# A decoder layer with a written-out instruction order: other priorities, and the rank-16 weights loaded later

## The chip, the core and the metric

The kernel runs on one core of a Trainium2 chip. Its time is the device time of one execution in microseconds (us); the median of several runs is compared. The engines of the core that matter here are TensorE (PE; its weight loads are listed as PEld), VectorE (DVE), ScalarE (ACT), GpSimd (POOL) and SyncE (SP), which only issues DMAs here. Each engine works through its own instructions strictly in order and waits at an instruction until the semaphores that it needs are there. ScalarE issues a few DMAs too, in line with its arithmetic.

## The reference

One decoder layer on x of 8 x 512 x 256 with a context of the same shape, in float32. Three blocks follow each other, each with a residual and a layer norm:

```python
x = layernorm(x + attn(x))            # chunked linear attention: chunks of 32, decay mask, sigmoid gate, W_o
x = layernorm(x + xattn(x, ctx))      # 16 heads of 64: softmax(q k^T / 8) v, then Wo + bo
x = layernorm(x + ffn(x))             # h = ternary(x, w_fc) + gate * (x v^T fast_b^T u^T); ternary(relu(h)^2, w_proj)
```

In the ffn, `v` is 16 x 256, `fast_b` 16 x 16, `u` 1024 x 16 and `gate` a number: the rank-16 path. The two ternary weight matrices are rounded to -1, 0 or 1 with a scale per row.

## The kernel before

**Number format.** Almost every matmul runs on float16 pairs: a float32 value is split into a high part (a cast, mostly on ScalarE) and a low part (a subtraction on VectorE or GpSimd), and three products (high-high, high-low, low-high) are added in PSUM.

**Stages.** The loop over the eight batches is flattened into 256 units `(b, p, qt)`: batch, head pair and a quarter of the 512 queries. For each unit, `scores` computes two heads' scores (tile `s`, two groups of half-row matmuls that run side by side), VectorE adds the mask and takes the row extremum (`nm`), and ScalarE exponentiates into `e`. `split_p` splits `e` into the high and low halves of `ph` (high on ScalarE or GpSimd, low on VectorE), and a DMA transpose on SP's queue turns two units' `ph` into `pT`. `attend` multiplies `pT` by the values into `av`, some four units later; after the fourth quarter, `of`, `oh` and a DMA transpose give `oT`.

Around the units other work is filled in by four fillers: `gen_kv`, `gen_q` and `gen_v` (tiles `pk`, `pq`, `pvv`, into `W` and `v`) for later head pairs; `gen_l0` for the first block of the next batch (`xa`, `pss`, `pv`, `pg`, `po`, `pp`, then layer norm, `xsa` and a DMA transpose to `x1T`); `load_ctx` (`ctxs` into `ctxh`, on GpSimd after batch 0); `gen_wo` and `gen_ffn` for the batch before (`pwo`, then `x2T`; `pz`, `ph` with a batch number, `r`, `rh`, `py`). At the boundary between two batches the new batch's `pk` and `pq` need `ctxh` and `x1T`, which GpSimd makes in the stretch in which it also makes the low halves `rh` of the ffn. The last batch ends in `wo_tail` (`pwl`) and two `ffn_tail` generators of 256 rows each (`pyl`, `rhl`), whose steps are interleaved by hand.

**The order.** The program is recorded, not issued: every operation becomes an `Op` with a priority (`prio`), the number of the unit beside which it was recorded plus an offset. `Recorder.schedule` (line 300) then simulates the engines with the durations of `cost` (line 254). At each free moment of an engine it takes the operation with the least priority whose inputs and buffers are ready; `REACH` (line 30) limits how far past the first ready candidate it looks, `STICK` and `HOLD` favour staying in half-row or full-row matmuls. The result is a fixed order for each engine. The offsets come from several tables: `LATE` by kind of work, `PULL` (how many matmuls a filler may add for each unit), `TP` (dates in the tail), and `OFF` (line 39), which adds an offset for an engine and the name of the written tile:

```python
        if self.prio >= 0 and outs:
            o.prio += OFF.get(engine + " " + re.split(r"[0-9_]", outs[0].t.name or "")[0], 0.0)
```

**Start and rank-16 weights.** At the start SP's queue loads `wqk`, `xs`, `w0s`, `ctxs`, `wqs`, rows and so on, while ScalarE's queue loads `ld`, `ident`, `dif`, `bq`, `bk`. `load_rank` (line 662, called at line 1249) has ScalarE's queue load `sv`, `ur`, `fb` and `gt` there too; `setup_ffn` (line 668) uses them in batch 0 to make `vst`, `uh`, `fbs`, `uT` and `ust`. All DMAs of both queues take their semaphores from one set of eight in turn, so an issue can wait until an earlier DMA has landed.

**Buffers.** Buffers come from rings: `pT` and `ph` (3 each, 128 x 4096 float16), `t4` (5), `tmp2` (4), and eight PSUM banks. In `ffn_tail` (line 1036) `rhl` for all eight steps is one whole `pT` or `ph` buffer.

Of the kernel before, what the change touches and what calls it, by code (L numbers as in the profile page):

```python
# [11 lines left out]
F16 = mybir.dt.float16  # L12
F32 = mybir.dt.float32
# [8 lines left out]
HID, RANK = 1024, 16  # L22
# [4 lines left out]
LAG = 4  # L27
BURST = 2
MARGIN = 0.0
REACH = 11.86  # L30
SPARE = 1
DLATE = 1.6
PTS = 3
PHS = 3
NWP = 4
TP = (-1.12, 2.0, 1.04, 3.04, 0.1, 5.1, 2.67)
STICK = 2.09
HOLD = 0.18
OFF = {"ACT th": -0.28, "ACT zst": -1.63, "ACT r": 0.81, "PE pTp": 1.99, "SP pT": 1.41, "ACT sph": 0.41, "DVE zf": 0.49, "PE ph": 0.16, "POOL ph": -1.37, "PE pwp": -0.46, "PE pTb": 2.45, "PE pb": 3.1, "POOL xh": 2.55, "ACT rh": 1.56, "PE pu": 0.39, "ACT row": 1.53, "PE po": -0.14, "PE pwl": 1.81, "SP xs": 0.62, "PE pss": -0.66, "DVE wqkv": -0.5, "DVE fct": -3.44, "ACT oh": -1.55, "DVE sp": 1.14, "POOL rhl": 0.12, "POOL oh": -0.82, "PE pyl": -0.58, "PE pz": -2.5, "PE pp": 0.13, "DVE mvb": -0.45}
HIGH = ("apaa", "paaa", "papp")  # L40
LATE = {"k": 0.0, "q": 0.0, "v": 0.53, "w": -0.48, "l": -0.41, "o": -0.91, "f": 0.31, "s": 0.0, "a": 0.91, "t": -0.55, "x": 0.31, "e": 0.0, "c": -1.28, "d": -0.95}
PULL = {"k": 4.41, "l": 2.62, "w": 3.61, "f": 4.71, "g": 4.5}

PASSES = ((0, 0), (0, 1), (1, 0))

# [109 lines left out]
class Recorder:  # L155
# [34 lines left out]
    def add(self, engine, method, args, kw):  # L190
        ins, outs = [], []
        for n, x in enumerate(args):
            if isinstance(x, View):
                (outs if n == 0 or (method == "tensor_tensor_reduce" and n == 7) else ins).append(x)
        for k, x in kw.items():
            if isinstance(x, View):
                (outs if k == "accum_out" else ins).append(x)
        o = Op()
        o.engine, o.method, o.args, o.kw, o.prio = engine, method, args, kw, self.prio
        if engine in ("DVE", "ACT") and method[:3] != "dma" and self.prio >= 0:  # L200
            src = ins[0].t if ins else None
            if method == "tensor_tensor_reduce":
                o.prio += LATE["t"]
            elif method == "activation" and args[2] == AF.Exp:
                o.prio += LATE["x"]
            elif src is not None and src.pool[:2] == "ps":
                o.prio += LATE["e"]
        if self.prio >= 0 and outs:
            o.prio += OFF.get(engine + " " + re.split(r"[0-9_]", outs[0].t.name or "")[0], 0.0)
        o.preds, o.succs, o.bufs, o.parts = {}, [], [], None  # L210
        self.cost(o, ins, outs)
        if self.joint is not None and self.joint:
            j = self.joint[0]
            j.parts.append(o)
            self.access(j, ins, outs)
            return o
        o.seq = len(self.ops)
        self.ops.append(o)
        self.access(o, ins, outs)
        if self.joint is not None:  # L220
            o.parts = [o]
            self.joint.append(o)
        return o
# [30 lines left out]
    def cost(self, o, ins, outs):  # L254

        n = max([int(np.prod(x.shape[1:])) for x in outs + ins] or [0]) if o.engine != "PE" else outs[0].idx.size
        psum = any(x.t.pool[:2] == "ps" for x in ins + outs)
        ones = sum(x.idx.size == 1 and x.t.free > 0 for x in ins)
        o.half, o.port = None, o.engine == "POOL"
        o.dma = o.method[:3] == "dma"  # L260
        if o.dma:
            x = (outs or ins)[0]
            if o.method == "dma_start_transpose":
                blocks = n / 128
                o.occ, o.lat = 0.1 * blocks + 0.4, 0.115 * blocks + 0.55
            else:
                size = {F32: 4, F16: 2}.get(x.t.dt, 1)
                o.occ, o.lat = 0.45, n * size * x.shape[0] / (380e3 if self.prio < 0 else 210e3) + (1.2 if size == 1 else 0.1)
        elif o.engine == "PE":
            o.occ = n / 2400 + 0.0025 if ins[0].t.dt is F16 else n / 200  # L270
            o.lat = o.occ + 0.17
            if ins[0].p1 - ins[0].p0 == 64:
                o.half = ins[0].p0
        elif o.engine == "DVE":
            lat = 0.145 + n * 1.042e-3
            if o.method == "tensor_tensor_reduce":
                o.occ, o.lat = 0.615, 0.8
                return
            if not psum and o.method in ("tensor_copy", "tensor_scalar") and n >= 512:
                lat = 0.12 + n * 0.62e-3  # L280
            if psum and ones and o.method == "scalar_tensor_tensor":
                lat += 0.065
            if n <= 8:
                lat = 0.19 if o.method == "reciprocal" else 0.175 if o.method == "bn_aggr" else 0.145
            o.occ, o.lat = lat - 0.085, lat
            o.port = not psum and o.method in ("tensor_tensor", "scalar_tensor_tensor", "tensor_scalar", "tensor_copy")
        elif o.engine == "ACT":
            lat = 0.165 + n * 0.83e-3 + (0.0 if psum else 0.04) + 0.07 * ones
            o.occ, o.lat = (lat + 0.01, lat + 0.12) if "accum_out" in o.kw else (lat - 0.11, lat)
        elif o.engine == "POOL":  # L290
            if o.method == "tensor_tensor":
                lat = 0.3 + n * 1.67e-3 if n <= 512 else 0.2 + n * 1.9e-3
                if o.args[3] == ALU.pow:
                    lat = 0.42 + 0.16 * n
            else:
                lat = 0.13 + n * 0.9e-3 if n > 512 else 0.92 if n == 256 and o.kw == {} and o.method == "tensor_scalar" and o.args[-1] == ALU.is_lt else 0.62 if n > 256 else 0.56 if n > 8 else 0.22 + n * 5e-3
            o.occ, o.lat = lat - 0.03, lat
# [178 lines left out]
def decoder_kernel(ctx: ExitStack, tc: tile.TileContext, ins: dict, out: bass.AP):  # L476
# [13 lines left out]
    def tmp2(name, shape, dt=F32):  # L490
        return wk.tile(shape, dt, tag="tmp2", name=name, bufs=4)
# [162 lines left out]
        nc.vector.tensor_scalar(th[:, 0:n], sc, 0.5, None, ALU.mult)  # L654
        nc.vector.tensor_scalar(th[:, n:2 * n], sc, -0.5, None, ALU.mult)

    sv = cst.tile([128, 2, RANK], F32, name="sv")
    ur = cst.tile([128, 8, RANK], F32, name="ur")
    fb = cst.tile([RANK, RANK], F32, name="fb")
    gt = cst.tile([128, 1], F32, name="gt")  # L660

    def load_rank():
        nc.scalar.dma_start(sv, ins["vT"].rearrange("(c p) r -> p c r", p=128))
        nc.scalar.dma_start(ur, ins["u"].rearrange("(c p) r -> p c r", p=128))
        nc.scalar.dma_start(fb, ins["fast_b"])
        nc.scalar.dma_start(gt, ins["gate"].broadcast_to([128, 1]))

    def setup_ffn():
        sfc = cst.tile([128, 8], F32, name="sfc")
        for i in range(2):  # L670
# [38 lines left out]
        yield 6  # L709

        nc.gpsimd.memset(vst, 0.0)
        split(vst[:, :, 0:RANK], vst[:, :, 96:96 + RANK], sv, WS)
        for g in (32, 64):
            nc.scalar.copy(vst[:, :, g:g + RANK], vst[:, :, 0:RANK])

        rs = cst.tile([128, 8], F32, name="rs")
        nc.vector.reciprocal(rs, sfc)
        nc.vector.tensor_scalar(rs, rs, gt, None, ALU.mult)
        nc.vector.tensor_tensor(ur, ur, rs.unsqueeze(2).broadcast_to([128, 8, RANK]), ALU.mult)
        uh = tmp2("uh", [128, 2, 8, RANK], F16)  # L720
        split(uh[:, 0], uh[:, 1], ur, 1.0)
        fbs = cst.tile([RANK, 2, 128], F16, name="fbs")
        nc.gpsimd.memset(fbs, 0.0)
        split(fbs[:, 0, 0:RANK], fbs[:, 1, 0:RANK], fb, 1.0)
# [311 lines left out]
    def ffn_tail(b, i, base, step_):  # L1036
        row = rows[b]
        rh, py = {}, {}
        ts = slice(256 * i, 256 * i + 256)

        rhl = wk.tile([128, 8, 2, 256], F16, tag=("pT", "ph")[i], name=f"rhl{i}", bufs=(PTS, PHS)[i])
        PL = 3
        for s_ in range(8 + PL):
            nc.prio = base + step_ * s_
# [2 lines left out]
            if s_ < 8:  # L1047
                j = s_
                r4 = ffn_h(b, j, ts, zst, f"{b}_{i}", True)
                hl = rhl[:, j]  # L1050
                if i == 0 or j % 2:
                    nc.scalar.activation(r4, r4, AF.Square)
                else:
                    nc.vector.tensor_tensor(r4, r4, r4, ALU.mult)
                if j % 2:
                    nc.scalar.copy(hl[:, 0], r4)
                else:
                    nc.vector.tensor_copy(hl[:, 0], r4)
                (nc.vector if j % 3 == 2 or (i == 1 and j == 7) else nc.gpsimd).tensor_tensor(hl[:, 1], r4, hl[:, 0], ALU.subtract)
                rh[j] = hl  # L1060
# [185 lines left out]
            setup_qkv(2, 0, N1, 0)  # L1246
            run_all(gen_v(0, 0))
    nc.prio = -1.0
    load_rank()
    for i in (1, 2, 0):  # L1250
        setup_qkv(i, N1, HID, 0)
    nc.prio = 0.0
# [3 lines left out]
    def at(i, off):  # L1256
        now[0], nc.prio = i, i + off
# [84 lines left out]
            if pend:  # L1342
                attend(pend.pop(0))

    at(U, TP[6])
    bf.drain()
    at(U, TP[0])
    rest(len(pend) - 4)
# [63 lines left out]
```

## Time and profile before

| | us |
|---|---|
| median of 3 runs (lowest, highest) | 1062.17 (1061.53, 1063.61) |
| profiled execution | 1060.95 |
| its span, first to last instruction | 1058.8 |
| PE, DVE, ACT, POOL busy | 994.6, 985.8, 884.5, 568.7 |
| idle of TensorE and VectorE, 548.2 to 671.9 (one batch) | 2.7, 6.6 |

The page gives busy time, share of the span and number of instructions of each engine, and slices of a fortieth of the span (26.5 us) whose digits are the busy share in tenths. A line of the timeline has start, duration, engine, source line, operation, output<-input and shapes, and in brackets the idle time before it with what ended that. Line 454 stands for every recorded operation, since all are issued there; tiles tell them apart. A busy TensorE is not one at its peak, because ends of pipelined matmuls are modelled.

### The profile page before, as it was taken

What the parts mean: (1) busy time and instruction counts of PE and PEld (TensorE: products, weight loads), DVE (VectorE), ACT (ScalarE), POOL (GpSimd) and SP (SyncE); (2) the same over time, 40 slices, a digit from 0 to 9 for tenths busy, and PEclk for the clock granted to TensorE, in tenths of its full rate; (3) what the DMA queues carried; (4) which work ended last, traced back from release to release, by engine and by line L of the source; (5) the groups of instructions that cost most, each with busy time, mean ns of one, the idle gap of its engine ahead of it and who ended that gap; (6) DMA issues with size and microseconds to landing.
All of it is one profiled execution on the core that took longest, in us unless ns stands there. A gap on an engine that the chain in (4) does not pass through costs nothing.

```text
span 1058.8 us, 29904 instructions
## 1 busy us (share of the span) xinstructions
PE 994.6 (94%) x11976; PEld 636.0 (60%) x11976; DVE 985.8 (93%) x2087; ACT 884.5 (84%) x1885; POOL 568.7 (54%) x518
## 2 busy tenths in 40 slices
PE   6987879999999999999999999999999999999996
PEld 4544545665666566765567656665567655565574
DVE  6998999999899989999899999999899998999886
ACT  6797978899986998789987899869987899878846
POOL 0255284256842587344952579425873449424646
PEclk9999999999999999999999999999999999999999
DMA  8359999999999999989999899999999899999971
GB/s 289 119 107 195 186 191 197 178 155 185 194 172 201 164 177 180 203 155 187 173 193 201 158 167 196 187 196 153 180 182 209 147 187 160 187 203 164 174 124 41
DMA packets 646635, 185.64 MB, mean 175 GB/s; under 512 B 628448, under 2 KB 641376, under 8 KB 646496
## 3 DMA queue, kind: packets, MB, share of 16 engines
q1 hardware_dynamic: 644144, 183.34, 94.5%
q8 instruction: 93, 1.52, 0.6%
q10 hardware_dynamic: 2352, 0.40, 0.2%
q14 instruction: 46, 0.38, 0.1%
HBM read 21.18 MB, written 4.19 MB: 24 GB/s over the span
## 4 chain that ended last, share of the span: by engine, by line
PE 48%; DVE 24%; POOL 8%; DMA 8%; ACT 5%; issue 5%; SPq 1%; ACTq 0%; POOLq 0%; DVEq 0%
PE s L454 9%; PE av L454 9%; DVE s L454 8%; DVE ph L454 6%; PE pwo L454 6%; PE pvv L454 5%; PE pk L454 4%; PE pq L454 4%; DMA pT<-ph 4%; PE py L454 3%; DVE W L454 2%; POOL xsa L454 2%; ACT e L454 2%; POOL row L454 2%; PE pxa L454 2%
## 5 line engine op out<-in xcount | busy, mean ns | idle before, releaser
L454 ACT ACTIVATE e<-s,nm 128x512 f32<-128x512 f32 x512 | 350.5, 696 | 79.8 <-DVE nm L454 72.2
L454 DVE SCALAR_TENSOR_TENSOR ph<-e,ph 128x1024 f16<-128x1024 f32 x256 | 334.6, 1310 | 22.7 <-ACT ph L454 20.5
L454 DVE CUSTOM_DVE_ANT_0 s<-s,mb 128x512 f32<-128x512 f32 x512 | 342.1, 706 | 11.0 <-PE s L454 10.0
L454 PEld LDWEIGHTS <-pT 128*128 128x128 f16 x6144 | 197.5, 98 | 60.6 <-issue 37.6
L454 PE MATMUL av<-v,pT 128*128 128x64 f16 x6144 | 212.3, 194 | 12.0 <-DMA pT<-ph 9.7
L454 PE MATMUL s<-W 64*128 64x512 f16 x1536 | 207.4, 379 | 10.7 <-ACT e L454 8.8
L454 ACT ACTIVATE ph<-e 128x1024 f16<-128x1024 f32 x186 | 198.2, 1071 | 2.0
L454 POOL TENSOR_SCALAR ph<-e 128x1024 f16<-128x1024 f32 x70 | 87.5, 1250 | 203.9 <-ACT e L454 187.7
L454 POOL TENSOR_TENSOR oh<-of,oh 128x512 f16<-128x512 f32 x62 | 99.3, 1602 | 92.3 <-ACT oh L454 86.6
L454 PEld LDWEIGHTS <-W 64*128 64x128 f16 x1536 | 64.6, 94 | 108.6 <-issue 53.9
L454 PEld LDWEIGHTS <-wqkv 128*128 128x128 f16 x768 | 68.6, 98 | 88.3 <-issue 27.2
L454 PE MATMUL pk<-ctxh,wqkv 128*128 128x512 f16 x384 | 97.9, 383 | 11.9 <-POOL ctxh L454 8.8
L454 ACT ACTIVATION_READ_ACCUMULATOR e<-s,nm 128x1 f32 x512 | 108.3, 211 | 0.0
L454 PE MATMUL pvv<-wqkv,ctxh 128*128 128x256 f16 x768 | 97.9, 274 | 0.2 <-ACT e L454 0.2
L454 PE MATMUL pq<-x1T,wqkv 128*128 128x512 f16 x384 | 96.1, 380 | 1.3 <-DVE x1T L454 0.7
L454 POOL TENSOR_TENSOR rh<-r,rh 128x512 f16<-128x512 f32 x56 | 76.1, 1367 | 21.2 <-ACT rh L454 20.7
L454 PEld LDWEIGHTS <-oT 128*128 128x128 f16 x768 | 73.4, 98 | 20.9 <-issue 4.8
L454 PEld LDWEIGHTS <-ctxh 128*128 128x128 f16 x768 | 72.8, 98 | 17.4 <-issue 5.9
L454 PE MATMUL pwo<-wo,oT 128*128 128x256 f16 x672 | 82.0, 273 | 0.8 <-ACT e L454 0.5
L454 DVE DVE_READ_ACCUMULATOR2_ANT nm<- 128x1 f32 x512 | 70.0, 137 | 0.0
L454 PE MATMUL ph<-x2T,tfc 128*128 128x512 f16 (+1 forms) x288 | 67.3, 355 | 0.3 <-DVE of L454 0.2
L454 PE MATMUL py<-tpj,rh 128*128 128x256 f16 x448 | 60.3, 273 | 1.3 <-ACT rh L454 1.2
(190 smaller groups left out, 1485.6 us busy)
## 6 DMA issues: line engine op xcount, KB each, us to landing
row<-in_x SPq DMA_DIRECT2D x8, 512.0 KB, 5.8
xs<-in_xT SPq DMA_DIRECT2D x7, 512.0 KB, 4.5
ctxs<-in_ctxT SPq DMA_DIRECT2D x7, 512.0 KB, 4.1
out_dram<-row SPq DMA_DIRECT2D x7, 512.0 KB, 3.5
wqs<-in_wqkv SPq DMA_DIRECT2D x6, 512.0 KB, 8.1
pT<-ph SPq DMA_TRANSPOSE x131, 7.6
wos<-in_wo SPq DMA_DIRECT2D x4, 256.0 KB, 3.2
fcs<-in_w_fc SPq DMA_DIRECT2D x2, 512.0 KB, 4.5
```

What stands on the lines that cost most here:

```text
L454: getattr(real[x.engine], x.method)(*[r(a) for a in x.args], **{k: r(a) for k, a in x.kw.items()})
```

## The change

The table `OFF` and its use go, so every operation's priority is that of its kind of work alone. `REACH`, `TP` (one date less; the drain of the fillers at the tail's start now is at unit number + 1 and not + 2.67), two entries of `LATE` and two of `PULL` get other values. `cost` no longer prices a float32 matmul apart. `load_rank` goes: `setup_ffn` loads `sv`, `gt`, `ur` and `fb` itself, on SP's queue, just ahead of their use in the program (where they land in the queue is up to the planner), `sv` and `ur` into `tmp2` buffers. The host lays `u` and `v` out per partition, so that each partition's values are one piece (512 and 128 bytes, before in pieces of 64 bytes). In `ffn_tail`, each step's `rhl` is a `t4` buffer of its own.

```diff
@@ -27,19 +27,18 @@
 LAG = 4
 BURST = 2
 MARGIN = 0.0
-REACH = 11.86
+REACH = 9.52
 SPARE = 1
 DLATE = 1.6
 PTS = 3
 PHS = 3
 NWP = 4
-TP = (-1.12, 2.0, 1.04, 3.04, 0.1, 5.1, 2.67)
+TP = (0.35, 0.96, 1.15, 3.0, 0.5, 5.1)
 STICK = 2.09
 HOLD = 0.18
-OFF = {"ACT th": -0.28, "ACT zst": -1.63, "ACT r": 0.81, "PE pTp": 1.99, "SP pT": 1.41, "ACT sph": 0.41, "DVE zf": 0.49, "PE ph": 0.16, "POOL ph": -1.37, "PE pwp": -0.46, "PE pTb": 2.45, "PE pb": 3.1, "POOL xh": 2.55, "ACT rh": 1.56, "PE pu": 0.39, "ACT row": 1.53, "PE po": -0.14, "PE pwl": 1.81, "SP xs": 0.62, "PE pss": -0.66, "DVE wqkv": -0.5, "DVE fct": -3.44, "ACT oh": -1.55, "DVE sp": 1.14, "POOL rhl": 0.12, "POOL oh": -0.82, "PE pyl": -0.58, "PE pz": -2.5, "PE pp": 0.13, "DVE mvb": -0.45}
 HIGH = ("apaa", "paaa", "papp")
-LATE = {"k": 0.0, "q": 0.0, "v": 0.53, "w": -0.48, "l": -0.41, "o": -0.91, "f": 0.31, "s": 0.0, "a": 0.91, "t": -0.55, "x": 0.31, "e": 0.0, "c": -1.28, "d": -0.95}
-PULL = {"k": 4.41, "l": 2.62, "w": 3.61, "f": 4.71, "g": 4.5}
+LATE = {"k": 0.0, "q": 0.0, "v": 0.53, "w": -0.33, "l": -0.41, "o": -0.91, "f": 0.31, "s": 0.0, "a": 0.91, "t": 0.0, "x": 0.31, "e": 0.0, "c": -1.28, "d": -0.95}
+PULL = {"k": 5.13, "l": 2.62, "w": 3.61, "f": 4.71, "g": 5.48}
 
 PASSES = ((0, 0), (0, 1), (1, 0))
 
@@ -205,8 +204,6 @@
                 o.prio += LATE["x"]
             elif src is not None and src.pool[:2] == "ps":
                 o.prio += LATE["e"]
-        if self.prio >= 0 and outs:
-            o.prio += OFF.get(engine + " " + re.split(r"[0-9_]", outs[0].t.name or "")[0], 0.0)
         o.preds, o.succs, o.bufs, o.parts = {}, [], [], None
         self.cost(o, ins, outs)
         if self.joint is not None and self.joint:
@@ -267,7 +264,7 @@
                 size = {F32: 4, F16: 2}.get(x.t.dt, 1)
                 o.occ, o.lat = 0.45, n * size * x.shape[0] / (380e3 if self.prio < 0 else 210e3) + (1.2 if size == 1 else 0.1)
         elif o.engine == "PE":
-            o.occ = n / 2400 + 0.0025 if ins[0].t.dt is F16 else n / 200
+            o.occ = n / 2400 + 0.0025
             o.lat = o.occ + 0.17
             if ins[0].p1 - ins[0].p0 == 64:
                 o.half = ins[0].p0
@@ -654,17 +651,6 @@
         nc.vector.tensor_scalar(th[:, 0:n], sc, 0.5, None, ALU.mult)
         nc.vector.tensor_scalar(th[:, n:2 * n], sc, -0.5, None, ALU.mult)
 
-    sv = cst.tile([128, 2, RANK], F32, name="sv")
-    ur = cst.tile([128, 8, RANK], F32, name="ur")
-    fb = cst.tile([RANK, RANK], F32, name="fb")
-    gt = cst.tile([128, 1], F32, name="gt")
-
-    def load_rank():
-        nc.scalar.dma_start(sv, ins["vT"].rearrange("(c p) r -> p c r", p=128))
-        nc.scalar.dma_start(ur, ins["u"].rearrange("(c p) r -> p c r", p=128))
-        nc.scalar.dma_start(fb, ins["fast_b"])
-        nc.scalar.dma_start(gt, ins["gate"].broadcast_to([128, 1]))
-
     def setup_ffn():
         sfc = cst.tile([128, 8], F32, name="sfc")
         for i in range(2):
@@ -709,16 +695,24 @@
         yield 6
 
         nc.gpsimd.memset(vst, 0.0)
+        sv = tmp2("sv", [128, 2, RANK])
+        nc.sync.dma_start(sv, ins["vT"].rearrange("p (c r) -> p c r", c=2))
         split(vst[:, :, 0:RANK], vst[:, :, 96:96 + RANK], sv, WS)
         for g in (32, 64):
             nc.scalar.copy(vst[:, :, g:g + RANK], vst[:, :, 0:RANK])
 
+        gt = cst.tile([128, 1], F32, name="gt")
+        nc.sync.dma_start(gt, ins["gate"].broadcast_to([128, 1]))
         rs = cst.tile([128, 8], F32, name="rs")
         nc.vector.reciprocal(rs, sfc)
         nc.vector.tensor_scalar(rs, rs, gt, None, ALU.mult)
+        ur = tmp2("ur", [128, 8, RANK])
+        nc.sync.dma_start(ur, ins["u"].rearrange("p (c r) -> p c r", c=8))
         nc.vector.tensor_tensor(ur, ur, rs.unsqueeze(2).broadcast_to([128, 8, RANK]), ALU.mult)
         uh = tmp2("uh", [128, 2, 8, RANK], F16)
         split(uh[:, 0], uh[:, 1], ur, 1.0)
+        fb = cst.tile([RANK, RANK], F32, name="fb")
+        nc.sync.dma_start(fb, ins["fast_b"])
         fbs = cst.tile([RANK, 2, 128], F16, name="fbs")
         nc.gpsimd.memset(fbs, 0.0)
         split(fbs[:, 0, 0:RANK], fbs[:, 1, 0:RANK], fb, 1.0)
@@ -1037,8 +1031,6 @@
         row = rows[b]
         rh, py = {}, {}
         ts = slice(256 * i, 256 * i + 256)
-
-        rhl = wk.tile([128, 8, 2, 256], F16, tag=("pT", "ph")[i], name=f"rhl{i}", bufs=(PTS, PHS)[i])
         PL = 3
         for s_ in range(8 + PL):
             nc.prio = base + step_ * s_
@@ -1047,7 +1039,7 @@
             if s_ < 8:
                 j = s_
                 r4 = ffn_h(b, j, ts, zst, f"{b}_{i}", True)
-                hl = rhl[:, j]
+                hl = t4(f"rhl{i}{j}", [128, 2, 256])
                 if i == 0 or j % 2:
                     nc.scalar.activation(r4, r4, AF.Square)
                 else:
@@ -1246,7 +1238,6 @@
             setup_qkv(2, 0, N1, 0)
             run_all(gen_v(0, 0))
     nc.prio = -1.0
-    load_rank()
     for i in (1, 2, 0):
         setup_qkv(i, N1, HID, 0)
     nc.prio = 0.0
@@ -1342,7 +1333,7 @@
             if pend:
                 attend(pend.pop(0))
 
-    at(U, TP[6])
+    at(U, 1)
     bf.drain()
     at(U, TP[0])
     rest(len(pend) - 4)
@@ -1391,8 +1382,8 @@
     a["bo"] = f("L0_xattn_bo").reshape(1, D)
     a["w_fc"] = f("L0_ffn_w_fc")
     a["w_proj"] = f("L0_ffn_w_proj")
-    a["u"] = f("L0_ffn_u")
-    a["vT"] = np.ascontiguousarray(f("L0_ffn_v").T)
+    a["u"] = np.ascontiguousarray(f("L0_ffn_u").reshape(8, 128, RANK).transpose(1, 0, 2).reshape(128, -1))
+    a["vT"] = np.ascontiguousarray(f("L0_ffn_v").T.reshape(2, 128, RANK).transpose(1, 0, 2).reshape(128, -1))
     a["fast_b"] = f("L0_ffn_fast_b")
     a["gate"] = f("L0_ffn_gate").reshape(1, 1)
     i = np.arange(128)
```

## The prediction

> **What bounds the kernel now.** I read the page's busy shares and slices first, then windows by stage, then the start and one batch boundary in the timeline.
>
> ```profile
> PE 994.6 (94%) x11976; PEld 636.0 (60%) x11976; DVE 985.8 (93%) x2087; ACT 884.5 (84%) x1885; POOL 568.7 (54%) x518
> PE   6987879999999999999999999999999999999996
> DVE  6998999999899989999899999999899998999886
> ```
>
> The slices have TensorE full from the seventh on; up to there VectorE is. The windows (us, then busy us of PE, PEld, DVE, ACT, POOL, clock, DMA share, GB/s) say how full:
>
> ```profile
> 48.00:92.00 44.00, 36.90 (x391) 20.79 (x389) 43.97 (x101) 38.14 (x92) 22.09 (x18) 0.97 0.66 120
> 92.00:164.00 72.00, 59.81 (x699) 35.19 (x696) 67.68 (x144) 56.69 (x123) 40.33 (x33) 0.97 1.03 192
> 1008.00:1027.00 19.00, 18.28 (x316) 15.92 (x314) 16.89 (x37) 8.93 (x22) 10.53 (x11) 1.00 0.92 149
> 1027.00:1058.80 31.80, 21.97 (x195) 16.23 (x191) 20.10 (x64) 20.23 (x51) 17.39 (x29) 0.95 0.10 34
> ```
> ```profile
> 548.20:671.90 123.70, 121.03 (x1481) 77.53 (x1479) 117.10 (x246) 106.34 (x223) 72.19 (x64) 1.00 1.03 181
> ```
>
> Batch 0 (to 164 us) is set by VectorE, the batches after it by TensorE. One such batch takes 123.7 us and TensorE stands still for 123.70 - 121.03 = 2.7 us of it; VectorE for 6.6. The tail is a chain with gaps on every engine. So a new order can win 2.7 us a batch at most, and lose more.
>
> **Part 1, the four rank-16 loads leave the start.** They are the last DMAs on ScalarE's queue, ahead of its table load:
>
> ```profile
> 5.05 0.39 ACTq L454 DMA_DIRECT2D sv<-in_vT  x1
> 6.91 1.28 ACT L454 ACT_TABLE_LOAD   x1 [6.91 <-DMA sv<-in_vT]
> 8.32 0.61 ACT L454 ACTIVATE wqkh<-wqk 128x512 f16<-128x512 f32 x1
> ```
>
> bk is issued at 2.62 and takes 0.45, so without sv, ur and fb the table load stands first at 3.07 and ends at 4.4; wqk lands 4.3 to 4.8 after its issue at 0.72, and wqkh can start at 5.1 to 5.5 instead of 8.32. The first matmul (9.88) follows 3 us sooner. The chain of waits has loads on the path next:
>
> ```profile
> 7.34 0.38 SPq L454
> ...
> 9.74 0.43 SPq L454
> ...
> 10.21 7.77 DMA wqs<-in_wqkv
> ```
>
> By the semaphores in the two instruction orders, each of these loads waits for the landing of the eighth DMA before it, counted over both queues. With four fewer in the count w0s waits for wqk and ident (5.1, 5.4) and no longer for wqk's second half and bq (6.0, 7.3), and the wqs that went out at 10.21 goes out near 8.7: 1.5 us sooner. VectorE is 27.72 of 28 us busy from 20 to 48 and 43.97 of 44 to 92, so what it gets sooner it keeps. Bounds -3.1 (ScalarE's step) and 0; I take -1.5, the load's step, because the chain runs through the load.
>
> **Part 2, the same loads later, on SP.** gt and fb go between two loads of rows that nobody awaits: 0. sv and ur are issued after the second tpj transpose, ahead of pT of head pair 3: two issues of 0.39 and 0.48 make +0.9. Behind sv on ScalarE stands the high half of ph (pair 4), behind ur on VectorE its low half; if landing (3.0 and 3.7 us at the start) isn't covered, both stand. Bounds 0 and +3.7; I take +0.8, as one score unit, a v and pwo work lie between. The layout in itself: ur's 64 KB landed in 3.7 us in pieces of 64 bytes; nobody waits for the bytes, 0. [...]
>
> **Part 3, batch 0 in another order.** The instructions are the same, and VectorE's work is. Its idle 4.3 us (92 to 164) is the most that can be won; as much again can be lost, since the largest TensorE stalls there are followed by a slow clock (below). No row tells which: 0, bounds -4 and +4. The planner's price for the one f32 matmul drops back; the trace has it as two of 0.39 us, once: 0.
>
> **Part 4, the batches in another order.** Without OFF, with REACH 9.52 and other PULLs, the two instruction orders differ in every batch alike. The work on TensorE is the same and so are the changes between half-row score groups and full-row groups (183 runs of scores before, 185 after). What differs is what lies between a result and its reader. At the boundary:
>
> ```profile
> 634.20 0.38 PE L454 MATMUL pk<-ctxh,wqkv 128*128 128x512 f16 x1 [0.50 <-POOL ctxh L454]
> 635.90 1.45 PE L454 MATMUL pk<-ctxh,wqkv 128*128 128x512 f16 x6 [1.22 <-POOL ctxh L454]
> ```
> ```profile
> PE pk L454 <- POOL ctxh L454: 1.7, 2, 1.2
> PEld L454 <- POOL rh L454: 1.0, 4, 0.4
> ```
>
> Before, one py matmul stands between pk's first matmul and the second; after, four ph, nine py, one pk and one pq do: 4 x 0.215 + 9 x 0.109 + 2 x 0.215 = 2.3 us, so the 1.2 and most of the 1.7 can go. Against that, py now follows its ph closer: from ph 4 to 7 to the py that reads them lie 9.2 to 10.1 us of matmuls, before 12.8 to 13.7 (by the same per-matmul times, 0.117 for a score matmul, 0.029 for av). Between them go relu, square and cast on ScalarE and a GpSimd subtraction of 1.2, and GpSimd is full there, with row (3.3), xsa (4.2), ctxh (3.5). At 13 us of cover the weight loads of py already waited 1.0 for rh. So a batch may win 1.7, or lose up to 3.6 of cover less the 1.2 = 2.4. I take +0.6, past the middle (+0.35), because x1T is also put ahead of a pT on SP's queue, and behind it stands the av that had 0.6 us to spare (pT issued at 630.54, landing 7.6 later, used at 638.7). Six boundaries with an ffn beside them: 6 x 0.6 = +3.6, bounds -10.2 and +14.4.
>
> **Part 5, the tail.** After the last score the old order still has 43 py matmuls of the batch before, the new one none: 4.1 us of matmuls less behind the last score and as much more ahead of it. Ahead, TensorE had 32 - 29.2 = 2.8 us idle (976 to 1008) to take it in. Behind, 18.28 of 19 us were busy, so most of it is won there. Net bounds -2.8 and +4.1; I take +0.5, near nothing. rhl moves from whole pT and ph buffers to five t4 buffers: rhl 15 on ScalarE now waits until pyl has read rhl 10, which is 11 pyl matmuls of 0.109 after ph 16, 1.2 us, of which one relu (0.42) covers a part: +0.7, bounds 0 and +1.2.
>
> **Sum.** -1.5 + 0.8 + 0 + 3.6 + 0.5 + 0.7 = +4.1 on the profiled execution's 1060.95 (span 1058.8 and 2.15 around it) gives 1065.1; the median of the runs is 1.2 above that execution, so 1066.3.
>
> **Rival 1, faster.** The wait for ctxh goes and the shorter cover for rh suffices: -0.7 a boundary, -4.2, with the start at -2 and the rest at 0: 1062.2 - 6.2 = 1056. For it: the boundary's wait is the largest that TensorE has in a batch, and the start's gain is plain in the trace. Against it: GpSimd is full exactly where the cover shrinks. It decides the other way once py waits more than 1.7 us a batch.
>
> **Rival 2, much slower.** The wait for rh or pT passes 2 us in each batch, and then the clock falls:
>
> ```profile
> 985.00:986.00 1.00, 0.43 (x4) 0.13 (x2) 1.00 (x1) 1.00 (x4) 1.00 (x2) 1.00 2.31 163
> 986.00:987.00 1.00, 0.00 (x0) 0.00 (x0) 1.00 (x2) 1.00 (x3) 1.00 (x1) 1.00 0.05 6
> 987.00:988.00 1.00, 0.53 (x11) 0.54 (x12) 1.00 (x4) 1.00 (x3) 0.66 (x1) 0.69 0.98 215
> 988.00:989.00 1.00, 1.00 (x10) 0.41 (x9) 0.07 (x2) 1.00 (x3) 0.93 (x1) 0.50 1.18 227
> ```
>
> About 2 us without a matmul, then 0.50 of the clock for some 3 us, that is 1.5 us lost. Six times 2.4 + 1.5 is 23 instead of 3.6: 1086; at three boundaries of six, 1076. [...] The row shows the drop after 2 us, so I keep the 1.5. Against it: the orders give every reader at least 9 us.
>
> **Rival 3, nothing to see.** The reordering is neutral and start and tail cancel: 1062.2, within the 0.2% (2.1 us) that a measurement of this kernel can tell from no change.
>
> **How the numbers follow.** Forecast (slower, 1064.3 to 1073) 0.56, rival 2 0.09, rival 1 0.27, rival 3 0.08. Hence slower 0.65, same 0.08, faster 0.27. The range for 8 in 10 reaches from rival 1's middle, 1056, to three boundaries of rival 2, 1076; the forecast's own range is 1063 to 1073.
>
> **What would show it.** Right or wrong, step by step: the table load near 3 us and the first pA matmul near 6.7; the chain's wqs issue near 8.7; no wait of pk for ctxh but longer ones of py, or PEld, for rh; a batch of 124.3 us where it was 123.7; no py after the last score, and ScalarE's rhl waiting for pyl. The prediction is wrong if a batch takes 123 us or less, or if idle time on TensorE in batch 0 moves by over 4 us.

## The result and the profile after

The changed kernel takes 1064.01 us (median of 22 runs), the one before 1062.13 on the same chip: ratio 1.0024, interval 1.0014 to 1.0033, that is 2.5 us slower (1.5 to 3.5). The ratio goes by all runs and is not the quotient of the two medians, which are 1.9 us apart. The forecast was 1066.3, slower. The profiled execution of the changed kernel took 1066.91 (span 1064.8), 2.9 above its median. Executions of one kernel lie up to some 5 us from its median, so below sizes come from these ratios with their intervals, each against the kernel before on the same chip, and profiles tell only where the time goes.

The page and the windows of the changed kernel, as they were shown of the kernel before:

```profile
PE 1003.9 (94%) x11976; PEld 641.8 (60%) x11976; DVE 985.0 (93%) x2087; ACT 882.3 (83%) x1885; POOL 555.8 (52%) x518
PE   7987878999999999999999999999999999998986
DVE  7999699999899989999899989999899998998976
```
```profile
92.00:164.00 72.00, 57.83 (x637) 32.65 (x637) 61.22 (x131) 51.47 (x115) 35.12 (x30) 0.88 0.95 177
548.40:672.10 123.70, 121.34 (x1487) 78.05 (x1484) 116.96 (x246) 106.08 (x223) 70.85 (x64) 1.00 1.04 182
1008.00:1027.00 19.00, 16.13 (x256) 13.02 (x253) 15.97 (x31) 7.98 (x22) 9.57 (x7) 0.91 1.13 188
```

Two places changed. In the fifth slice (106 to 133 us) VectorE falls from 9 to 6 tenths; from 92 to 164 us it now idles 72 - 61.22 = 10.8 us where it idled 4.3, and the clock is 0.88, not 0.97. And near the end TensorE has two slices at 8 (958 to 985 and 1011 to 1038 us) where all but the last were full. The stretch of 123.7 us in the steady batches looks as before; it has the length that one batch had before, and by the units below a batch of the changed kernel is shorter, 122.7 us on average for 123.4.

Where the time is gained and lost is read best from the order of the units. The table gives the start (us) of VectorE's first masking step `s<-s,mb` of some units, counted in the trace of each profiled execution; the kernels are those of the experiments below.

| first step of unit | 0 | 16 | 24 | 32 | 64 | 224 | 255 | end of span |
|---|---|---|---|---|---|---|---|---|
| before | 49.5 | 110.6 | 136.9 | 167.4 | 285.1 | 902.0 | 1010.4 | 1058.8 |
| after | 46.0 | 108.4 | 143.1 | 171.7 | 290.2 | 903.5 | 1013.5 | 1064.8 |
| e5 | 50.4 | 114.7 | 144.7 | 176.7 | 298.8 | 915.0 | 1023.5 | 1072.1 |
| e6 | 46.0 | 108.2 | 141.1 | 169.8 | 288.2 | 903.2 | 1011.5 | 1062.8 |
| e7 | 44.4 | 112.8 | 141.9 | 174.4 | 297.7 | 909.1 | 1017.8 | 1068.9 |
| e8 | 47.5 | 108.4 | 134.7 | 165.4 | 282.2 | 897.4 | 1006.0 | 1057.4 |
| f | 48.0 | 109.3 | 135.7 | 166.0 | 285.6 | 903.3 | 1011.5 | 1060.1 |

After against before: 3.5 us ahead at unit 0, 4.3 behind at unit 32, with 8.4 lost between units 16 and 24 alone (34.7 us for 26.3); from unit 64 to 224, five batches, 613.3 for 616.9; from unit 255 to the end 51.3 for 48.4. So the change seems to gain at the start and in the steady batches and to lose in batch 0 and in the tail; these are single executions, and the experiments say how much of it holds.

**The start** went as the prediction's Part 1 had it (timeline of the changed kernel, ScalarE and TensorE):

```profile
3.11 1.28 ACT L451 ACT_TABLE_LOAD   x1 [3.11 <-issue]
...
4.99 0.63 ACT L451 ACTIVATE wqkh<-wqk 128x512 f16<-128x512 f32 x1
...
6.63 0.59 PE L451 MATMUL pA<-wqkh,wqkh 128*128 128x256 f16 x2 [6.63 <-ACT wqkh L451]
```

The table load is at 3.11 instead of 6.91, the first matmul at 6.63 instead of 9.88, and the first decay step on VectorE (`sp`) 2.4 us sooner.

**Batch 0** has a hole. The chain of waits of the changed kernel runs through SP's queue there, and VectorE's timeline shows who stands:

```profile
107.82 1.28 SPq L451
...
109.20 3.29 DMA sv<-in_vT
```
```profile
109.05 0.73 DVE L451 CUSTOM_DVE_ANT_0 s<-s,mb 128x512 f32<-128x512 f32 x1
109.70 0.14 DVE L451 DVE_READ_ACCUMULATOR2_ANT nm<- 128x1 f32 x1
112.77 0.19 DVE L451 SCALAR_TENSOR_TENSOR vst<-sv,vst 128x32 f16<-128x32 f32 x1 [2.93 <-ACT vst L451]
```

The late `sv` is issued at 109.20, behind a transpose, and lands 3.29 us later; ScalarE and VectorE stand at `vst` until then, with `ph` of a unit queued behind it. VectorE stands for 2.93 us, and a slow clock follows (0.57, then 0.50); the load is not the whole of it, since in e6 below, where `sv` is early, VectorE still stands 1.04 us at this step, for ScalarE. Windows of 1 us, changed kernel (columns as in the prediction; the clock is the third number from the end):

```profile
109.00:110.00 1.00, 0.38 (x4) 0.10 (x1) 0.84 (x4) 0.71 (x3) 0.00 (x0) 1.00 2.54 149
110.00:111.00 1.00, 0.00 (x0) 0.00 (x0) 0.00 (x0) 0.73 (x3) 0.00 (x0) 1.00 0.06 7
111.00:112.00 1.00, 0.70 (x24) 0.71 (x25) 0.00 (x0) 0.00 (x0) 0.00 (x0) 1.00 0.81 167
112.00:113.00 1.00, 1.00 (x27) 1.00 (x24) 0.19 (x1) 0.49 (x2) 0.00 (x0) 0.57 0.74 160
...
121.00:122.00 1.00, 1.00 (x7) 0.47 (x6) 0.78 (x4) 0.84 (x3) 0.72 (x1) 0.50 0.00 0
122.00:123.00 1.00, 1.00 (x21) 0.78 (x20) 0.00 (x0) 1.00 (x4) 0.00 (x0) 0.80 0.00 0
```

TensorE stood for 1.92 us (to 111.30, for a `pT` transpose) and the clock was 0.57 and then 0.50 until 122.

**The steady batches.** The waits from 290 to 905 us, before and after:

```profile
PE pk L454 <- POOL ctxh L454: 8.1, 9, 1.2
...
PEld L454 <- POOL rh L454: 4.4, 18, 0.4
...
PE py L454 <- ACT rh L454: 1.0, 4, 0.3
```
```profile
PE pk L451 <- POOL ctxh L451: 3.1, 5, 0.7
```

The wait of `pk` for `ctxh` fell from 8.1 to 3.1 us, and the shorter way from `ph` to `py`, which the prediction feared, costs nothing: no wait of `py` for `rh` is left, nor of the weight loads for GpSimd's `rh` (for ScalarE's half they still wait 1.0 us in all, 2.4 before).

### The profile page after: what moved, and what is told of

Its sections match the earlier page's. It is cut to its first block, busy times and chain, and to the rows that moved or that the text cites. A ratio compares the mean times of both kernels' runs of the same rounds, so it can differ in the third digit from the quotient of the medians.

```text
span 1064.8 us, 29936 instructions
## 1 busy us (share of the span) xinstructions
PE 1003.9 (94%) x11976; PEld 641.8 (60%) x11976; DVE 985.0 (93%) x2087; ACT 882.3 (83%) x1885; POOL 555.8 (52%) x518
## 4 chain that ended last, share of the span: by engine, by line
PE 38%; DVE 22%; ACT 16%; DMA 12%; issue 6%; POOL 3%; SPq 2%; POOLq 0%; DVEq 0%; ACTq 0%
PE s L451 8%; PE av L451 7%; DMA pT<-ph 7%; DVE ph L451 6%; DVE s L451 6%; ACT e L451 5%; ACT r L451 4%; PE pk L451 4%; PE pwo L451 3%; PE pq L451 3%; PE pvv L451 3%; PE py L451 3%; ACT ph L451 2%; DVE W L451 2%; SPq L451 2%
## 5 line engine op out<-in xcount | busy, mean ns | idle before, releaser
L451 ACT ACTIVATE e<-s,nm 128x512 f32<-128x512 f32 x512 | 354.2, 704 | 100.1 <-DVE nm L451 88.6
L451 PEld LDWEIGHTS <-pT 128*128 128x128 f16 x6144 | 200.6, 99 | 61.3 <-issue 30.6
L451 PE MATMUL av<-v,pT 128*128 128x64 f16 x6144 | 214.8, 195 | 14.3 <-DMA pT<-ph 14.1
L451 PE MATMUL s<-W 64*128 64x512 f16 x1536 | 209.8, 382 | 13.2 <-ACT e L451 11.2
L451 POOL TENSOR_SCALAR ph<-e 128x1024 f16<-128x1024 f32 x70 | 85.0, 1214 | 209.5 <-ACT e L451 208.2
L451 PEld LDWEIGHTS <-W 64*128 64x128 f16 x1536 | 64.2, 94 | 112.8 <-issue 61.2
L451 POOL TENSOR_TENSOR oh<-of,oh 128x512 f16<-128x512 f32 x62 | 89.4, 1443 | 74.6 <-ACT oh L451 74.6
L451 ACT ACTIVATION_READ_ACCUMULATOR e<-s,nm 128x1 f32 x512 | 112.5, 220 | 0.0
L451 PE MATMUL pk<-ctxh,wqkv 128*128 128x512 f16 x384 | 101.7, 379 | 5.3 <-POOL ctxh L451 4.5
L451 PE MATMUL pvv<-wqkv,ctxh 128*128 128x256 f16 x768 | 102.6, 275 | 0.6 <-ACT e L451 0.6
```

The lines of the kernel that those rows point to most:

```text
L451: getattr(real[x.engine], x.method)(*[r(a) for a in x.args], **{k: r(a) for k, a in x.kw.items()})
```

## The experiments

**The changed kernel with tiles of their own for sv and ur (e1).**

```diff
-        sv = tmp2("sv", [128, 2, RANK])
+        sv = cst.tile([128, 2, RANK], F32, name="sv")
-        ur = tmp2("ur", [128, 8, RANK])
+        ur = cst.tile([128, 8, RANK], F32, name="ur")
```

> The changed kernel, but sv and ur in buffers of their own instead of tmp2, so that the planner can put their two loads early on SP's queue, beside gt and fb. Theory A (the late loads cost batch 0: in the changed kernel ScalarE and VectorE wait for sv near 109 us, VectorE idles 8.3 us from 104 to 128 and TensorE's clock is 0.51 from 112 to 120): 4 to 6 us less than the changed kernel, about 1059. Rival B (batch 0 loses through its new order, the loads are beside the point): within 1.5 us of the changed kernel, about 1064.

1067.73 us, ratio to before 1.0047 (1.0031 to 1.0064): slower than the changed kernel itself. With two tiles fewer in the `tmp2` ring the planner ordered the rest of batch 0 anew, and units 0 to 32 took 128.8 us. So it did not test the loads; e6 does.

**Only the four loads moved (e2).** The kernel before with its order pinned on every engine; the loads of `sv`, `ur`, `fb`, `gt` go later on ScalarE's own queue, with the `vst` and first `fbs` steps that read them.

```diff
+        for o in ops:   # n: name of the tile written
+            if o.prio < 0 and o.dma and n and n[0] in ("sv", "ur", "fb", "gt"):
+                o.start = PIN[0]      # just behind m8_0
+            elif o.engine == "ACT" and n and (n[0] == "vst" or n[0] == "fbs" and o.start < PIN[1]):
+                o.start = PIN[1]      # just behind ScalarE's last wo
         ops.sort(key=lambda o: (o.start, o.seq))
```

> The kernel before with its planned order kept on every engine, except that the issues of sv, ur, fb and gt and ScalarE's first steps on them come later on ScalarE (after the mask's load; after wo's splits). Theory A (the early loads hold back the start, VectorE is full until 92 us and keeps what it gets): first pA matmul at 6.6 instead of 9.9, 1.5 to 2.5 us less than the kernel before, about 1060. Rival B (the loads of wqs and the waits of batch 0 swallow it): within 0.7 us of the kernel before, although the first matmul comes 3 us sooner.

1059.98, ratio 0.9977 (0.9963 to 0.9990): -2.4 us. The first matmul starts at 6.55, and the head start reaches the end.

**Only the steady order (e3).** The kernel before with the changed tables for units 32 to 223.

```diff
-        if self.prio >= 0 and outs:
+        if self.prio >= 0 and outs and not alt(self.prio):   # alt: 32 <= prio < 224; OFF elsewhere only
-                o.prio += LATE["t"]
+                o.prio += 0.0 if alt(self.prio) else LATE["t"]
-                        if pick is not None and x[0] > pick[0] + REACH:
+                        if pick is not None and x[0] > pick[0] + (9.52 if alt(pick[0]) else REACH):
...
+   PULL "k" is 5.13 for these units
```

> The kernel before with the changed kernel's offsets, REACH, LATE t and PULL k for units 32 to 223 alone (batches 1 to 6); start, batch 0 and tail keep the tables of before. Theory A (the new steady order is the better one, 122.8 us a batch for 123.7, because pk no longer waits for ctxh): 4 to 7 us less than the kernel before, about 1056. Rival B (the batches differ by what batch 0 hands over, or the new order costs as the prediction had it): no gain, 1062 to 1066.

1058.07, ratio 0.9958 (0.9936 to 0.9980): -4.5 us. The new order of the batches is the better one, and the sign of the prediction's largest term was wrong.

**Only the tail (e4).** The kernel before with the changed tables from unit 224 on, `TP`, PULL `g`, and `rhl` in `t4` buffers.

> The kernel before with the changed kernel's tables from unit 224 on (last batch and tail), its TP, PULL g and the t4 buffers for rhl. Theory A (the last batch and tail lose in the new order: TensorE runs out of work between 1016 and 1020 and again near 1034, and its clock falls): 4 to 7 us more than the kernel before, about 1067. Rival B (the profiled execution of the changed kernel was a late one, 2.9 us above its median, and the excess is there): 1 to 2 us more.

1061.13, ratio 0.9989 (0.9978 to 1.0001): no loss seen here. Its profile does show one: from unit 224 to the end it took 158.3 us. Over all fourteen profiles this stretch takes 158.3 to 161.3 us in the seven kernels with the changed tables there, and 156.3 to 157.8 in the seven with those of before. See e8 and f.

Start, steady batches and tail, measured apart, so add up to -8, and the whole is +2.5: batch 0 had to be taken apart.

**Only the order of batch 0 (e5).** As e3, but for units 0 to 31 (with LATE `w` -0.33); the loads stay early.

> The kernel before, with the changed kernel's tables (no offsets, REACH 9.52, LATE t 0 and w -0.33, PULL k 5.13) in batch 0 alone (units 0 to 31); the rank-16 loads stay early on ScalarE's queue, batches 1 to 7 and the tail keep the tables of before. Theory Z (what the change loses, it loses by the order of batch 0 itself): start -2.4, steady batches -4.5 and tail -1 were measured apart and sum to -8, the change as a whole is +2 to +2.5, so batch 0 must cost 8 to 10: 1069 to 1073 against 1062.5 of before. Rival L (the late loads on SP's queue cost it, through the hole at 104 to 128 us): nothing here, 1061 to 1064.

1073.84, ratio 1.0103 (1.0078 to 1.0128): +11. Units 0 to 32 took 126.3 us, before 117.9. But 4.4 more were lost from unit 32 to 64 (122.1 for 117.7), where the two sets of tables meet, a seam that the changed kernel does not have. A seam need not cost: e3 and e8 have one at the same unit and took 117.1 and 116.8 there. Why this one does was not settled.

**The changed kernel, order pinned, only sv and ur early (e6).** Every engine's order but SP's is that of the changed kernel; `sv` and `ur` get tiles of their own (lines left out below).

```diff
+        EARLY = <start of the first pjs load> + 1e-3
+        for o in ops:
+            if o.dma and <o writes sv or ur>:
+                o.start = EARLY
         ops.sort(key=lambda o: (o.start, o.seq))
```

> The changed kernel with the order of every engine as it is, only sv and ur are loaded earlier on SP's queue (behind the first pjs load, at 40 us instead of 109), into tiles of their own. Rival L: the stretch 104 to 128, in which VectorE stood still for 8.3 us, closes by 4 to 6, and the run is at 1058 to 1060 against 1064 of the changed kernel. Theory Z: vst comes sooner but the steps behind it wait for the transposes that stand in the same queue; the run is at 1062 to 1065.

1062.46, ratio 1.0002 (0.9986 to 1.0017), against 1.0024 of the changed kernel: 2.3 us, with both intervals 0.4 to 4.2. In its trace VectorE's step on `vst` starts at 110.67 for 112.77, and the scores before it at 108.84 for 109.05, so 1.9 of the 2.1 us arise here. So the late loads cost about that; what e6 still lacks is in batch 0's order and the tail.

**The changed kernel with the tables of before in batch 0 (e7).** The mirror of e5: `OFF`, REACH 11.86, LATE `t` and `w` and PULL `k` of before for units 0 to 31, the loads late.

> The changed kernel with the tables of before in batch 0 alone (offsets, REACH 11.86, LATE t -0.55 and w -0.48, PULL k 4.41 for units 0 to 31); the rank-16 loads stay late on SP's queue. Theory Z: the loss of batch 0 goes, 1055 to 1058. Rival L: the late loads still cost it, 1062 to 1065.

1073.87, ratio 1.0101 (1.0085 to 1.0116): neither theory. Units 0 to 32 took 130.0 us, and the seam 5.6 more. So it is not the tables of before as such that are good for batch 0; the one order that they gave, with the early loads and everything else as it was, is. VectorE from 92 to 164 us in three kernels, e8 (order of before), e5 and e6 (windows, columns as above):

```profile
92.00:164.00 72.00, 60.95 (x726) 35.18 (x725) 67.98 (x146) 57.48 (x124) 40.57 (x33) 0.95 1.06 192
```
```profile
92.00:164.00 72.00, 55.86 (x615) 31.81 (x612) 62.59 (x133) 52.16 (x112) 33.68 (x27) 0.88 0.87 167
```
```profile
92.00:164.00 72.00, 58.74 (x657) 33.28 (x657) 62.95 (x132) 52.29 (x117) 37.04 (x32) 0.91 0.95 180
```

VectorE idles 4.0 us where batch 0 has the order of before, and 9.0 to 9.4 in two other orders whose `sv` and `ur` are early; the clock is lower there too (0.88 and 0.91 against 0.95). In all, the order of before ran units 0 to 32 in 117.8 to 118.9 us in the nine kernels that have it (before, e2, e3, e4, e8 and those below), four other orders (after, e1, e5, e7) in 125.7 to 130.0, and e6, that of after with early loads, in 123.8.

**The gaining parts together (e8).** The loads of e2, batch 0 in the order of before, the changed tables from unit 32 to the end.

> The parts that gained, together: the kernel before with batch 0 in its own order, the rank-16 loads moved behind the first m8 on ScalarE's queue (e2), and the changed kernel's tables from unit 32 to the end, tail and rhl buffers included (e3 and e4). If the parts add up: 1062.7 - 2.7 - 4.6 - 1.5 = 1053.9, so 1052.5 to 1056. Rival (the head start is lost again when the order of the batches is another, as batch 0 ends later or VectorE and not TensorE sets the boundary to batch 1): 1057 to 1059.

1060.58, ratio 0.9984 (0.9971 to 0.9997): faster than before, but only by 1.7 where -8.8 was hoped for.

**e8 without the tail (f).** Tables of before, and its `rhl` buffers, from unit 224 on.

> The kernel before with the pinned order of e2 (rank-16 loads later on ScalarE's queue) and the changed kernel's tables for units 32 to 223 alone; from unit 224 on the tables and rhl buffers of before. Theory T (the tables from unit 224 on cost what e8 lacked: in the profiles the stretch from the last unit's scores to the end took 50.6 to 51.4 us in all six kernels with them and 48.4 to 50.6 in the four without): 1055 to 1058, at least 2 below e8's 1060.6. Rival (the shortfall of e8 is not in the tail, the gains of e2 and e3 do not add): 1059 to 1061.

1057.46, ratio 0.9958 (0.9944 to 0.9972): -4.5 us, the best kernel here with e3. The tail costs the difference to e8, 0.26% or 2.8 us (0.8 to 4.8). The gains of e2 and e3 do not add in full here, -4.5 for both and not -6.9, but the 2.4 between them is known to some 3 us only, so this is not clear of noise.

Where the tail loses is seen on TensorE (timelines of the changed kernel, of e8 and of f; in each the 73rd to 96th av matmul after the last scores, in f as part of the 42):

```profile
1020.00 1.42 PE L451 MATMUL av<-v,pT 128*128 128x64 f16 x24 [2.04 <-DMA pT<-ph]
```
```profile
1012.16 0.96 PE L467 MATMUL av<-v,pT 128*128 128x64 f16 x24 [1.68 <-DMA pT<-ph]
```
```profile
1014.31 1.26 PE L467 MATMUL py<-tpj,rh 128*128 128x256 f16 x10
1015.41 1.39 PE L467 MATMUL av<-v,pT 128*128 128x64 f16 x42
```

With no `py` left behind the last score, `av` waits 2.04 and 1.68 us for its transpose, and in e4 the next group of `av` 2.06. In f, as before, 50 `py` stand behind the last scores, and this `av` does not wait. The windows of the changed kernel add what follows:

```profile
1016.00:1020.00 4.00, 1.24 (x27) 0.73 (x24) 2.66 (x6) 0.78 (x2) 3.07 (x2) 1.00 1.19 131
1020.00:1024.00 4.00, 3.92 (x58) 3.48 (x59) 2.47 (x5) 1.21 (x3) 0.00 (x0) 0.57 1.17 239
```

TensorE works 1.24 us of 4, and then at 0.57 of the clock. That the missing `py` are the whole of the tail's loss is argued from these lines; no kernel had them alone put back.

**e8 with rhl in whole buffers (g), and the kernel before with rhl in t4 buffers (h).** The edit is that of h; g is e8 without it.

```diff
-        rhl = wk.tile([128, 8, 2, 256], F16, tag=("pT", "ph")[i], name=f"rhl{i}", bufs=(PTS, PHS)[i])
...
-                hl = rhl[:, j]
+                hl = t4(f"rhl{i}{j}", [128, 2, 256])
```

> e8 with rhl in whole pT and ph buffers as before: of the tail only the tables TP, PULL g and the missing offsets are the changed kernel's. If the five t4 buffers cost the tail 1 to 2 us (ScalarE waits for pyl at rhl 15): 1058.5 to 1059.8, and the stretch from the last unit's scores to the end is 49 to 50. Rival (the buffers cost nothing, the order does): 1060.6 as e8, stretch 51.

> The kernel before with rhl in t4 buffers alone; every engine's order is the same as before. The prediction's term: +0.7 (0 to 1.2), so 1062.7 to 1063.9, and ScalarE waits for pyl in the tail by up to 1.2. Rival: nothing, the five buffers suffice, 1062.7 and no such wait.

g: 1060.49, ratio 0.9981 (0.9964 to 0.9998), as e8. h: 1062.46, ratio 0.9997 (0.9985 to 1.0009), every engine's order as before. The buffers cost nothing either way, and no wait of ScalarE for `pyl` is in any of these traces. The tail's loss is the order.

**Only the offsets gone (i).** The kernel before without `OFF` for units 32 to 223.

> The kernel before without the offsets per kind (OFF) for units 32 to 223 alone; REACH, LATE and PULL stay as before. If the offsets are what made the steady order slower: 1058 to 1060, near e3's 1058.1, and TensorE's waits of pk for ctxh fall. Rival (it is REACH and the PULLs): 1061.5 to 1064.

1061.17, ratio 0.9992 (0.9982 to 1.0002): -0.8, not e3's -4.5. The waits of `pk` for `ctxh` over the whole run fell as far as in e3 (2.8 us; e3 3.9; before 8.8), but another came. TensorE from unit 64 to 224, i and then e3:

```profile
PEld L459 <- DMA pT<-ph: 8.4, 11, 1.3
...
PE av L459 <- DMA pT<-ph: 3.9, 10, 0.8
```
```profile
PEld L459 <- DMA pT<-ph: 5.7, 9, 1.4
...
PE av L459 <- DMA pT<-ph: 2.1, 3, 1.0
```

With REACH, LATE `t` and PULL `k` still as before, weight loads and `av` wait for `pT` instead. Taking out the offsets alone is not what wins; the other values without that were not tried.

## Why the prediction was right, and where its steps were not

The direction and the range held: 1064.0 against 1066.3, within 1056 to 1076. The size was high, +4.1 against +2.5 (1.5 to 3.5), and 1064.0 still lies within the 2.1 us of rival 3; only the many runs tell it from no change. The sum did not hold term by term. That the total came near is luck: the largest term had the wrong sign, and three terms that were too small made up for much of it.

| term | predicted | measured | by |
|---|---|---|---|
| start | -1.5 (-3.1 to 0) | -2.4 (-3.9 to -1.1) | e2 |
| late loads | +0.8 (0 to +3.7) | +2.3 (0.4 to 4.2) | after less e6 |
| order of batch 0 | 0 (-4 to +4) | +1.9 (-0.2 to 4.1) | e6 less e8 |
| batches | +3.6 (-10.2 to +14.4) | -4.5 (-6.8 to -2.1) | e3 |
| batches, with the early start | | -2.0 (-4.1 to 0.1) | f less e2 |
| tail | +0.5 (-2.8 to +4.1) | +2.8 (0.8 to 4.8) | e8 less f |
| rhl buffers | +0.7 (0 to 1.2) | -0.3 (-1.6 to 1.0) | h |
| sum | +4.1 | +0.1 with e3, +2.5 with f less e2 | |

The measured sums leave out h, because e8 less f holds the `rhl` buffers too. From the kernel before over e2, f, e8 and e6 to the changed kernel is one chain of steps, so with f less e2 for the batches the sum is the whole, 2.5 (2.6 with the rounding of the rows), by construction and proves nothing. With e3 in its place it lacks 2.4 us, just what e2 and e3 lack in f. Noise can make that much; whether start and batches truly fail to add was not settled.

**Start.** Both dates came (3.11 and 6.63). The four wqs issues began at 7.69 instead of 9.26, the 1.5 us sooner that the step named. The step was sized by the loads' step alone; the measured -2.4 lies between that and ScalarE's bound of -3.1, and its interval holds both.

**Late loads.** The mechanism was right: the steps behind `sv` on both engines stood. The term was too small because the cover that it named, a score unit, a v and pwo, was no cover: these steps are ahead of the wait on TensorE, and VectorE had run out of scores by 109.84. It stood 2.93 us where it stands 1.04 with the load early, and what follows came 1.9 us later, not 0.8.

**Batch 0.** The bound failed in the profile: idle time of VectorE rose by 10.8 - 4.3 = 6.5 us, and in e6, without the late loads, by 9.0 - 4.3 = 4.7, not 4 at most, for "as much again can be lost" was no bound at all. The sign that the prediction named, TensorE's idle time, would have missed it: from 92 to 164 us it moved from 12.2 to 14.2 only. In e5 and e7 other orders of batch 0 lost 11 us, seam included. The ratios give the order alone +1.9, not clear of zero, and the single profiles of e6 and e8 from unit 0 to 32 give 123.8 - 117.9 = 5.9. What in the order costs it is not pinned to one instruction.

**Batches.** The failed step is the choice of +0.6 a boundary out of -1.7 to +2.4. Its first half was right, the `ctxh` wait fell by more than half. The second half was wrong: 9.2 to 10.1 us of matmuls between ph and py suffice for relu, square, cast and the subtraction, since no `py` waits. e3 makes -4.5 / 6 = -0.75 a boundary, near rival 1's -0.7; f less e2 makes -0.3. In the profiles the eight kernels with the new order take 614.2 us on average from unit 64 to 224 and the five with the old one 616.5, some -0.4 a batch. In i the `ctxh` wait fell as far with only -0.8 us gained, so that wait by itself is not the whole gain. The sentence that the prediction is wrong if a batch takes 123 us or less names it: five batches took 613.3, 122.7 each, in one execution.

**Tail.** That no `py` stands after the last score was right. The trace has 50 of them before and not 43; less 12 `pwp` that now stand there, 38 x 0.109 makes the 4.1 us of matmuls. Taken as work that is merely done sooner, they were booked at nearly nothing. By the lines above they were the cover of a transpose. The one sentence that a cover's removal needs, who is late next, was missing. e4 shows the same wait in its trace and yet no loss in its time, and this stays open.

**rhl.** Five buffers suffice; no wait came.

**Rival 2** had its mechanism in the wrong place. No boundary stalled for 2 us (from 164 to 960 us `pk` waits 0.7 us at most), but batch 0 and the tail stood for about that long, and a slow clock followed: the rows show 0.57 and then 0.50 after a gap of 1.92 us, and a mean of 0.57 in the 4 us after one of 2.04.

## What to carry to other kernels

Before a cover is removed or work is moved ahead of a wait, look for what landed under it, and price that. A schedule that came out of a planner is worth what its one order is worth: changing a ring, a load or a table elsewhere gives batch 0 another order, so test a part with the order pinned, and do not count on parts to add. A total that comes out right is no evidence for its terms: here terms of wrong size and one of wrong sign made it. And steps that lead in a chain from one kernel to the other always add up to the whole, so such a sum is no check.

## What the runs showed of the hardware

The length of a gap alone did not tell whether the clock fell. In the changed kernel TensorE stood for 2.04 us up to 185.42, for a `pT` transpose, and the clock stayed at 1.00 for the 10 us behind it; after the 2.04 us up to 1020.00 it was 0.55 in the next microsecond and 0.50 in the two behind it. Nor did the longer gap bring the fall sooner: in e6 TensorE stood longer at the place of batch 0's hole than in the changed kernel (2.30 us, to 111.47, against 1.92), and the clock stayed full for some 5 us more (windows of e6):

```profile
110.00:111.00 1.00, 0.00 (x0) 0.00 (x0) 0.33 (x2) 1.00 (x4) 0.00 (x0) 1.00 0.07 7
...
116.00:117.00 1.00, 0.52 (x5) 0.11 (x3) 1.00 (x4) 1.00 (x4) 1.00 (x2) 1.00 0.03 8
117.00:118.00 1.00, 0.89 (x5) 0.28 (x4) 0.13 (x2) 1.00 (x4) 1.00 (x2) 0.56 0.01 1
...
120.00:121.00 1.00, 1.00 (x21) 0.80 (x19) 0.00 (x0) 1.00 (x4) 0.02 (x1) 0.73 0.00 0
```

There it was slow for some 3 us, in the changed kernel for some 10, while TensorE was busy 0.36 to 1.00 of each microsecond. What sets the date and the length was not tried.
